# GNN layer and FFN in one kernel: outer weights loaded by rows, phase 3's opening in a fixed order, unused transposes in FFN's first waits, chunk 0's layernorm by two engines

## The chip, the core and the metric

One core of one Trainium2 chip runs the whole program. The metric is the device time of one execution in microseconds (us); the median of three runs is compared. TensorE (PE) multiplies and transposes, VectorE (DVE), ScalarE (ACT) and GpSimd (POOL) do elementwise work, SyncE (SP) issues most DMAs. All data are 32-bit floats; a matmul of such data shows as two records on PE, a transpose as one.

## The reference

`x` has 10000 rows (nodes) of 512, and there are 5000 edges with 64 attributes each.

```python
edge_index = jnp.stack([src, dst])
x = x + gnn(layernorm(x), edge_attr_64, edge_index, W_e, b_e, W1, ...)
x = x + ffn(layernorm(x)[None], controller, f1, f2)[0]

def gnn(x, edge_attr, ...):
    msg = relu(x[src] + edge_attr @ W_e + b_e)
    h = (1.0 + eps) * x + segment_sum(msg, dst, num_segments=x.shape[0])
    h = silu(bn(h @ W1 + b1, g1, beta1))          # 512 -> 1024
    h = h @ W2 + b2                               # 1024 -> 512
    return silu(bn(h, g2, beta2))                 # bn: over all nodes, per column

def ffn(x, controller, f1, f2):                   # groups of 16 tokens, 16 experts x 4 sets
    logits = einsum('bgtd,des->bgtes', grouped, controller) + tie
    perm = (logits == max over the 16 tokens)     # one token per group, expert and set
    inner = relu(einsum over t of (grouped @ f1) with perm)      # f1: 512 x (64 * 32)
    return einsum('bgesd,bgtes->bgtd', inner @ f2, perm)         # f2: (64 * 32) x 512
```

## The kernel before, in words

*Phase 1* (to about 200 us) gathers the edges' source rows, computes messages and adds them to `agg` in HBM. *Phase 2* (to 744 us) computes `h @ W1` for ten pairs of 500-node blocks, *phase 3* (to 1228 us) `h @ W2` for the same ten pairs, *FFN* (to the end) works on 20 chunks of 512 nodes.

Both products are done by Strassen's scheme with seven products instead of eight: `weight_sums` makes five sums of weight quarters (u1, u2, u5, u6, u7) on DVE, `block_sums` makes sums of data quarters (s1, s3, s6 on POOL, s4, s7 on DVE), and `strassen` runs products 1 to 7 for one output block `m`, each over `kb` pieces (2 in phase 2, 4 in phase 3), in PSUM banks x, w, z, y, v; products 6 and 7 add to the banks of 3 and 1. Products 2 and 5 read the data itself and u2 and u5; 3 and 4 read w2 itself and s3 and s4. The order of the products is a tuple (`FIRST`, (2, 5, 4, 3, 1, 6, 7), for the first output block of a phase).

Between phase 2 and 3 stands batchnorm 1. Phase 2's last pair keeps its four result pieces in SBUF (`xt`, `at`); phase 3 starts with this pair. For each piece `m`, `bn1` aggregates the statistics (bn_aggr on DVE), takes the root (two operations on POOL) and makes scale and shift (three on DVE), and ACT applies SiLU in place (L420). Piece 3 is the last to be ready. The weight sums for phase 3 read `w2` (L106, w_u in the profile). The other nine pairs are loaded from `h1s` in HBM, into `hc` or into `xt` and `at`.

In FFN a chunk's four tiles of 128 tokens go through these steps: `load_y` (yt, from `h2s`), `load_x`, `silu` (ACT, on yt), `residual` (four transposes of yt on PE into a bank, an addition on DVE), `stats` (bn_stats and bn_aggr on DVE), `norm` (four small operations on POOL, then per tile one scaling into `xl`, on POOL), `flip` (transposes of xl, a copy by ACT to `xlt`), `logits`, `choose` (three DVE operations), `by_token` (two transposes, then products into `bd` on DVE), `gather` (PE, copied by ACT to `gs`), `inner` (PE, with the inner weights `f1`), `relu`, and one step later `outer` (PE, with the outer weights `f2`), `turn` (DVE transposes) and `scatter`. A function `step` writes one order for four chunks at a time: `a` is at flip to by_token, `b` at gather to relu, `d` at outer, `e` at turn and scatter; `n1`, `n2` are the next two. `InOrder` keeps every operation of an engine in the program's order, so FFN's order is the one that is written; in phases 2 and 3 a scheduler places what is not marked with `keep_in_program_order`. A pool's tile is free again when its last reader is done: that decides when a load may be issued. SP issues its DMAs one after the other. All of FFN's operations on the engines show as L529, so the trace is read by tiles there. yt and x of chunk 0 are loaded early into a pool of their own; the other FFN tiles lie where phase 3's were.

FFN begins with `load_y`, `load_x` and `silu` of chunks 0 and 1, the loads of f1, then residual and stats of chunk 0, its norm, three residuals of chunk 1, and `step` for chunk 0 alone. Then the loads of f2 follow, in eight parts of 32 partitions:

```python
for q in range(2):
    for h in range(2):
        for t in range(2):
            rows = slice(64 * q + F * h, 64 * q + F * (h + 1))
            nc.sync.dma_start(out=f2_to[rows, :, t, :], in_=f2[h, q, :, :, t, :])
```

Of the kernel before, what the change touches and what calls it, by code (L numbers as in the profile page):

```python
# [20 lines left out]
EPS = 1e-5  # L21

P = 128
# [22 lines left out]
NP = NB // 2  # L46
FIRST = (2, 5, 4, 3, 1, 6, 7)


@with_exitstack  # L50
def gnn_ffn_kernel(ctx: ExitStack, tc: tile.TileContext, a: dict, out: bass.AP):
# [24 lines left out]
    def batchnorm(name, stats, blocks, g, beta):  # L76


        mv = const.tile([P, blocks, 2], F32, name=name + "_mv")
        sc = const.tile([P, blocks], F32, name=name + "_sc")  # L80
        sh = const.tile([P, blocks], F32, name=name + "_sh")

        def part(ms):
            for m in range(blocks)[ms]:
                nc.vector.bn_aggr(out=mv[:, m, :], in_=stats[:, m, :, :].rearrange("p c s -> p (c s)"))
            x = sc[:, ms]
            nc.gpsimd.tensor_scalar(x, mv[:, ms, 1], EPS, None, op0=ALU.add)
            nc.gpsimd.tensor_tensor(x, x, power[:, ms, 0], ALU.pow)
            nc.vector.tensor_mul(x, x, g[:, ms])
            nc.vector.tensor_mul(sh[:, ms], mv[:, ms, 0], x)  # L90
            nc.vector.tensor_sub(sh[:, ms], beta[:, ms], sh[:, ms])

        return sc, sh, part
# [4 lines left out]

    def weight_sums(pool, name, w, kb, mh):

        def q(i, j):
            return w[:, j * kb:(j + 1) * kb, i * mh:(i + 1) * mh]

        def f(n, x0, x1, op):
            t = pool.tile([P, kb, mh], F32, name=f"{name}_u{n}")
            tc.keep_in_program_order(nc.vector.tensor_tensor(t, x0, x1, op))  # L106
            return t

        u2 = f(2, q(1, 0), q(1, 1), ALU.add)
        u5 = f(5, q(0, 0), q(0, 1), ALU.add)  # L110
        u1 = f(1, q(0, 0), q(1, 1), ALU.add)
        u7 = f(7, q(0, 1), q(1, 1), ALU.subtract)
        u6 = f(6, q(1, 0), q(0, 0), ALU.subtract)
        return {1: u1, 2: u2, 3: q(0, 0), 4: q(1, 1), 5: u5, 6: u6, 7: u7}

    def block_sums(pool, name, kb, q):


        r = {n: [q(i, i, k, k + 1)[:, 0] for k in range(kb)] for n, i in ((2, 0), (5, 1))}
        for n, eng, x0, x1, op in ((3, nc.gpsimd, (0, 1), (1, 1), ALU.subtract),  # L120
                                   (1, nc.gpsimd, (0, 0), (1, 1), ALU.add),
# [4 lines left out]
            r[n] = [t[:, k, :] for k in range(kb)]  # L126
            for k0, k1 in [(0, kb)] if q(0, 0, 0, kb) is not None else [(k, k + 1) for k in range(kb)]:
                eng.tensor_tensor(t[:, k0:k1], q(*x0, k0, k1), q(*x1, k0, k1), op)  # L128
        return r

    def strassen(ps, tmp, us, bs, kb, m, res, bias0, bias1, y, order=(3, 1, 2, 5, 4, 6, 7)):


        banks, kept, done = {}, {}, set()

        def product(n, bank, start):
            for k in range(kb):
                nc.tensor.matmul(bank, lhsT=us[n][:, k, m * P:(m + 1) * P], rhs=bs[n][k],  # L138
                                 start=start and k == 0, stop=k == kb - 1, skip_group_check=True)

# [4 lines left out]
        def part(name, x0, sc, x1, op, dst=None):  # L145
            if dst is None:
# [9 lines left out]
                ({4, 5, 7}, lambda: part(None, 7, bias0, "t1", ALU.add, res[:, 0, 0, :]))]  # L156
        names = {2: ("w", 1), 5: ("v", 1), 4: y, 3: ("z", 2), 1: ("x", 2)}
        for n in order:
            if n in names:
                banks[n] = ps.tile([P, TB], F32, name=names[n][0], bufs=names[n][1])  # L160
# [176 lines left out]
    with tc.tile_pool(name="p2", bufs=1) as p2, tc.tile_pool(name="ps_2", bufs=1, space=PSUM) as ps_2:  # L337
# [86 lines left out]
        for i in range(NP):  # L424
# [4 lines left out]
            for m in range(4):  # L429
# [15 lines left out]
                else:  # L445

                    bn1(slice(m, MH, 4))
                    for r, t in ((0, slice(0, 2)), (1, slice(0, 2))) if m < 3 else (
                            (0, slice(0, 1)), (1, slice(1, 2)), (1, slice(0, 1)), (0, slice(1, 2))):
                        silu(h1[:, r, t, :].rearrange("p t n -> p (t n)"), 4 * r + m)  # L450
                if more and 0 < m < 3:
# [12 lines left out]
    with tc.tile_pool(name="pb", bufs=1) as pb, tc.tile_pool(name="ps_3", bufs=1, space=PSUM) as ps_3:  # L464
        u2 = weight_sums(pb, "w2", w2, 4, H // 2)
        for o, i in enumerate([NP - 1, *range(NP - 1)]):
            if o > 0:
# [4 lines left out]
                for m in range(4):  # L472
                    for r in range(2):
                        silu(pieces[m][:, r].rearrange("p t n -> p (t n)"), 4 * r + m)
            bs = block_sums(pb, "h", 4, lambda r, t, k0, k1: pieces[k0][:, r, t:t + 1, :] if k1 == k0 + 1 else None)
            for m in range(2):
                h2 = pb.tile([P, 2, 2, TB], F32, name="h2", bufs=2)
                strassen(ps_3, pb, u2, bs, 4, m, h2, b2[:, m:m + 1], b2[:, 2 + m:3 + m], ("y", 2),
                         *((FIRST,) if o == m == 0 else ()))
                for r in range(2):  # L480
# [12 lines left out]
    for t in range(2):  # L493
        for u in range(4):
            for b in range(2):
                nc.vector.tensor_copy(
                    ctl.rearrange("p k (t u q s b) -> p t u b k q s", t=2, u=4, q=2, s=2)[:, t, u, b],
                    ctl_in.rearrange("p k (u b q t s) -> p t u b k q s", t=2, u=4, q=2, s=2)[:, t, u, b])

# [33 lines left out]
    class Chunk:  # L533
# [61 lines left out]
        def norm(self):  # L595
# [8 lines left out]
            for j, (_, m, _) in enumerate(self.tiles):  # L604
                xl = pf.tile([P, H], F32, name="xl", bufs=8)
                pool.tensor_scalar(xl[:m, :], self.row_tile(j)[:m, :], self.rs[:m, j, :], self.sh[:m, j, :],
                                        op0=ALU.mult, op1=ALU.add)
                self.xl.append(xl)
# [73 lines left out]
        def inner(self, k, gs):  # L682
# [5 lines left out]
            for m in range(MF):  # L688
                for q in range(2):
                    b, t = m // 2, m % 2  # L690
                    j = 4 * b + 2 * q + t
                    pe.matmul(self.pi[64 * q:64 * q + 64, m], lhsT=f1_sb[:, k, 2 * F * j:2 * F * (j + 1)],
# [107 lines left out]
    def step(a, b, d, e, n1, n2):  # L800
# [36 lines left out]
        def silu(k):  # L837
            if n1 and n1.c == 2:
                n1.silu(k)
            if n2 and n2.c > 2:  # L840
                n2.silu(k)

        m1 = n1 if n1 and n1.c > 1 else None
        put(m1, Chunk.load_x)
        put(e, Chunk.split)
# [38 lines left out]
        lo(3)  # L884
        put(a, Chunk.choose)
        res(m1, 0)
        put(d, Chunk.outer, 2)
        res(m1, 1)
        put(a, Chunk.by_token)
        put(d, Chunk.outer, 3)  # L890
        stats(m1, 0)
# [10 lines left out]
    for k in range(KH):  # L902
        nc.sync.dma_start(out=f1_sb[:, k, :], in_=a["L0_ffn_f1"][k * P:(k + 1) * P, :])
    for j in range(4):
        chunks[0].residual(j)
        chunks[0].stats(j)
    chunks[0].norm()
    for j in range(3):
        chunks[1].residual(j)
        if j < 2:  # L910
            chunks[1].stats(j)
    step(at(0), None, None, None, at(1), at(2))

    f2 = a["L0_ffn_f2"].rearrange("(b q t s f) d -> s q f b t d", s=2, q=2, t=2, f=F)
    f2_to = f2_sb.rearrange("p (b t) d -> p b t d", t=2)
    for q in range(2):
        for h in range(2):
            for t in range(2):
                rows = slice(64 * q + F * h, 64 * q + F * (h + 1))
                nc.sync.dma_start(out=f2_to[rows, :, t, :], in_=f2[h, q, :, :, t, :])  # L920
    for c in range(1, NC):
# [96 lines left out]
```

## Time and profile before

| | us |
|---|---|
| median of 3 runs (lowest, highest) | 1945.13 (1942.31, 1946.38) |
| the profiled execution: time, span | 1945.13, 1943.3 |
| PE busy | 1798.0 (93%) |
| DVE busy | 1200.9 (62%) |
| ACT busy | 720.9 (37%) |
| POOL busy | 628.9 (32%) |
| mean granted clock of TensorE | 0.969 |

The span runs from the first to the last instruction; what lies around it is 1.8 us. In the 40 slices of the page each digit is the busy share of a slice (48.6 us) in tenths; PEclk is the granted clock in tenths of full speed. "idle before <-X" names the engine and line that ended a wait, inferred from semaphores. PEld are weight loads, which overlap matmuls.

### The profile page before, as it was taken

Reading aid. Unit: us, or ns where it says so; the run is one execution under the profiler, and the core shown is the slowest. Engines: PE = TensorE matmul, PEld = TensorE weight load, DVE = VectorE, ACT = ScalarE, POOL = GpSimd, SP = SyncE. Lnnn points to the kernel's source line nnn. Section 1 sums busy time; section 2 is a strip of 40 time slices with the busy share of each in tenths; the row PEclk is TensorE's granted clock in tenths of the full one; section 3 lists DMA queues with packets and bytes.
Section 4 is the critical chain, followed back from the end, with each engine's and each line's share of the span. In section 5 each row is a group of like instructions: output and inputs, shape, how many; then the busy total and the mean of one; then the engine's idle time right before and its main releaser. Section 6 shows DMA issues by size and latency. Waiting matters only on the chain.

```text
span 1943.3 us, 43938 instructions
## 1 busy us (share of the span) xinstructions
PE 1798.0 (93%) x19354; PEld 1032.9 (53%) x19354; DVE 1200.9 (62%) x1904; ACT 720.9 (37%) x970; POOL 628.9 (32%) x638
## 2 busy tenths in 40 slices
PE   4969499999999997999999999789999999999997
PEld 2424244444444443444444444466867677777764
DVE  7536367777777767343433334416878786868777
ACT  0324233333333233222222220255656555555543
POOL 4275433333233224333333332122232323232332
PEclk9979699999999998999999999789999999999999
DMA  9997444443444312333333331652232323323101
GB/s 349 304 233 144 109 172 171 162 162 148 162 162 163 145 43 85 127 148 126 127 136 139 127 127 42 212 157 68 90 111 90 108 93 101 100 97 94 58 25 58
DMA packets 95217, 256.35 MB, mean 132 GB/s; under 512 B 7845, under 2 KB 8435, under 8 KB 94452
## 3 DMA queue, kind: packets, MB, share of 16 engines
q1 hardware_dynamic: 86068, 232.58, 32.8%
q0 software_dynamic: 8960, 20.98, 5.4%
q8 instruction: 151, 2.47, 0.5%
q14 instruction: 38, 0.31, 0.1%
HBM read 143.47 MB, written 110.07 MB: 130 GB/s over the span
## 4 chain that ended last, share of the span: by engine, by line
PE 68%; DVE 10%; DMA 7%; ACT 5%; POOL 4%; SPq 3%; issue 2%; POOLq 0%; DVEq 0%; ACTq 0%
PE pb L529 16%; PE pi L529 10%; PE x L138 9%; PE z L138 9%; PE w L138 5%; PE v L138 5%; PE ps L529 4%; PE y L138 3%; SPq L217 3%; PE pc L309 2%; DVE ln_st L360 2%; ACT xt L371 2%; DVE st L442 2%; DMA L_ffn_controller_sb<-in_L_ffn_controller_dram 2%; ACT it L529 2%
## 5 line engine op out<-in xcount | busy, mean ns | idle before, releaser
L138 PE MATMUL x<-h_s,w_u 128*128 128x500 f32 x640 | 287.9, 582 | 0.3 <-POOL h_s L128 0.3
L529 ACT COPY gs<-pb 128x1024 f32<-128x1024 f32 (+2 forms) x168 | 161.6, 1027 | 120.1 <-PE pb L529 115.6
L138 PEld LDWEIGHTS x<-h_s,w_u 128*128 128x128 f32 x640 | 121.5, 190 | 147.3 <-issue 142.3
L529 DVE STREAM_TRANSPOSE it<-it 128x1024 f32<-128x1024 f32 x152 | 175.0, 1210 | 0.1
L529 PE MATMUL pi<-gs,f_sb 128*64 128x64 f32 x5120 | 167.4, 226 | 0.9 <-issue 0.9
L529 PEld LDWEIGHTS pi<-gs,f_sb 128*64 128x64 f32 x5120 | 158.7, 141 | 8.9 <-issue 1.9
L529 PE MATMUL pb<-bd,xl 32*128 32x128 f32 x2504 | 145.4, 287 | 12.6 <-ACT it L529 8.8
L529 POOL TENSOR_TENSOR pv<-perm,odd_t 64x512 f32<-64x512 f32 (+1 forms) x80 | 99.9, 1248 | 174.9 <-PE pb L529 152.6
L148 DVE SCALAR_TENSOR_TENSOR t<-w,s 128x500 f32<-128x500 f32 x60 | 40.7, 678 | 183.9 <-PE w L138 176.4
L138 PE MATMUL z<-h_s,w 128*128 128x500 f32 x320 | 147.6, 583 | 4.1 <-POOL h_s L128 4.1
L138 PE MATMUL z<-h_s,w_u 128*128 128x500 f32 x320 | 144.0, 582 | 0.3 <-POOL h_s L128 0.3
L529 PEld LDWEIGHTS pb<-bd,xl 32*128 32x128 f32 x2504 | 129.8, 189 | 25.2 <-ACT it L529 13.6
L529 DVE COPY it<-pb 128x1024 f32<-128x1024 f32 x72 | 88.2, 1225 | 83.4 <-PE pb L529 83.4
L529 PE MATMUL pb<-f_sb,ib 32*32 32x256 f32 x4864 | 132.5, 385 | 6.8 <-ACT it L529 4.7
L128 POOL TENSOR_TENSOR h_s<-hc 128x500 f32<-128x500 f32 x60 | 77.0, 1318 | 152.0 <-PE z L138 152.0
L529 ACT COPY it<-pb 128x1024 f32<-128x1024 f32 x76 | 79.6, 1047 | 104.1 <-PE pb L529 104.1
L143 ACT COPY s<-z 128x500 f32<-128x500 f32 x60 | 34.5, 575 | 213.8 <-PE z L138 164.6
L529 POOL TENSOR_SCALAR ln_rs<-ln_mv 128x4 f32<-128x4 f32 (+2 forms) x22 | 5.0, 226 | 304.1 <-DVE ln_mv L529 294.2
L138 PEld LDWEIGHTS z<-h_s,w_u 128*128 128x128 f32 x320 | 60.7, 190 | 74.0 <-issue 72.2
L128 POOL TENSOR_TENSOR h_s<-hb 128x1000 f32<-128x1000 f32 x30 | 69.6, 2335 | 87.0 <-PE z L138 65.3
L442 DVE BATCH_NORM_STATS2 st<-h 128x6 f32<-128x500 f32 x144 | 93.7, 671 | 1.3
L529 PEld LDWEIGHTS pb<-f_sb,ib 32*32 32x32 f32 x4864 | 68.8, 103 | 45.8 <-issue 12.8
(190 smaller groups left out, 3118.7 us busy)
## 6 DMA issues: line engine op xcount, KB each, us to landing
h1s<-h SPq DMA_DIRECT2D x36, 1000.0 KB
agg<-zero SPq DMA_DIRECT2D x10, 2048.0 KB
xt<-in_x_dram SPq DMA_DIRECT2D x20, 1000.0 KB
hc<-h1s SPq DMA_DIRECT2D x20, 1000.0 KB
h2s<-h SPq DMA_DIRECT2D x20, 1000.0 KB
x<-in_x_dram SPq DMA_DIRECT2D x39, 512.0 KB
out_dram<-x SPq DMA_DIRECT2D x39, 512.0 KB
yt<-h2s SPq DMA_DIRECT2D x76, 256.0 KB
```

Source lines behind the costliest of these rows:

```text
L128: eng.tensor_tensor(t[:, k0:k1], q(*x0, k0, k1), q(*x1, k0, k1), op)
L138: nc.tensor.matmul(bank, lhsT=us[n][:, k, m * P:(m + 1) * P], rhs=bs[n][k], start=start and k == 0, stop=k == kb - 1, skip_group_check=True)
L143: nc.scalar.copy(kept[n], banks[n])
L148: nc.vector.scalar_tensor_tensor(dst, banks[x0], sc, kept[x1], op0=op, op1=ALU.add)
L217: nc.sync.dma_start(out=agg[r0:r0 + j * P, :].rearrange("(p j) d -> p j d", j=j), in_=zero.to_broadcast([P, j, H]))
L309: nc.tensor.matmul(pc, lhsT=same[k][:, i, :], rhs=xgs[g * EG + k], start=(k == i), stop=(k == EG - 1))
L360: tc.keep_in_program_order(nc.vector.bn_stats(out=st[:RT, j, :], in_=self.xt[:RT, j, :]))
L371: keep(nc.scalar.activation(r, r, AF.Identity, bias=self.sh[:RT, j, :], scale=self.rs[:RT, j, :]))
L442: nc.vector.bn_stats(out=st1[:, 4 * r + m, 2 * i + t, :], in_=h1[:, r, t, :])
L529: return lambda *args, **kw: tc.keep_in_program_order(f(*args, **kw))
```

## The change

- *Outer weights*: f2 is loaded as it lies, 128 rows to the 128 partitions, in four DMAs of 1 MB. The place of two indices (set bits t and q) is swapped in `ctl` and in `inner`, so that the inner results stand in the order of these rows.
- *Phase 3's opening*: the sums for the first three pieces, then u2 and u5, then batchnorm's small operations and SiLU for piece 3, then the other sums, then u1, u7, u6 are written in this order. For the first output block TensorE runs products 4, 3, 2, 5 on three pieces each, then on the fourth piece each, then 1, 6, 7.
- *Unused transposes*: `keep_going(n)` transposes the identity n times into a bank that nobody reads: 24 ahead of chunk 0's first residual, 4 behind each of the seven residuals, 8 behind choose and 6 behind by_token of chunk 0.
- *Chunk 0's layernorm*: the scaling of tiles 1 and 3 is done by ACT, that of 0 and 2 by POOL.
- *Chunk 2*: x is loaded ahead of f2 (it was behind), and its four SiLUs stand ahead of step 1 (they stood amid it, one each before those of chunk 3).

```diff
+LATER = (4, 3, 2, 5, 1, 6, 7)
...
-        def part(ms):
...
+        def root(ms, keep=lambda x: x):
...
+        def rest(ms, keep=lambda x: x):
...
-    def weight_sums(pool, name, w, kb, mh):
+    def weight_sums(pool, name, w, kb, mh, between=lambda: None):
...
         u5 = f(5, q(0, 0), q(0, 1), ALU.add)
+        between()
         u1 = f(1, q(0, 0), q(1, 1), ALU.add)
...
+        def rest():
+            for n in (3, 1, 4, 6, 7):
+                for eng, *args in todo[n]:
+                    f = eng.tensor_tensor(*args)
+                    if between:
+                        tc.keep_in_program_order(f)
+
+        if between:
+            for n in (3, 4):
+                while len(todo[n]) > 1:
+                    eng, *args = todo[n].pop(0)
+                    tc.keep_in_program_order(eng.tensor_tensor(*args))
+            between(rest)
...
+        for n in order[:early]:
+            banks[n] = ps.tile([P, TB], F32, name=names[n][0], bufs=names[n][1])
+            product(n, banks[n], True, range(kb - 1))
         for n in order:
-            if n in names:
+            if n in banks:
+                product(n, banks[n], False, [kb - 1])
+            elif n in names:
...
+                    else:
+                        bn1.root(slice(m, MH, 4), tc.keep_in_program_order)
...
+            def last_block():
+
+                bn1.rest(slice(3, MH, 4), tc.keep_in_program_order)
+                for r, t in ((0, 0), (1, 1), (1, 0), (0, 1)):
+                    silu(pieces[3][:, r, t, :], 4 * r + 3)
+                others()
...
-                         *((FIRST,) if o == m == 0 else ()))
+                         *((LATER, 4) if o == m == 0 else ()))
...
-                    ctl_in.rearrange("p k (u b q t s) -> p t u b k q s", t=2, u=4, q=2, s=2)[:, t, u, b])
+                    ctl_in.rearrange("p k (u b t q s) -> p t u b k q s", t=2, u=4, q=2, s=2)[:, t, u, b])
...
+                if self.c == 0 and j % 2:
+                    act.activation(xl[:m, :], self.row_tile(j)[:m, :], AF.Identity, bias=self.sh[:m, j, :],
+                                   scale=self.rs[:m, j, :])
...
-                    j = 4 * b + 2 * q + t
+                    j = 4 * b + 2 * t + q
...
-            if n1 and n1.c == 2:
-                n1.silu(k)
...
-        put(m1, Chunk.load_x)
+        if m1 and m1.c > 2:
+            m1.load_x()
...
         put(a, Chunk.choose)
+        if a and a.c == 0:
+            keep_going(8)
...
         put(a, Chunk.by_token)
+        if a and a.c == 0:
+            keep_going(6)
...
+    def keep_going(n):
+
+        idle = ps_b.tile([P, 2, 2, HD], F32, name="pb")
+        for i in range(n):
+            pe.transpose(idle[:, 0, 0, :P], ident, ident)
+
+    keep_going(24)
     for j in range(4):
         chunks[0].residual(j)
         chunks[0].stats(j)
+        keep_going(4)
     chunks[0].norm()
     for j in range(3):
         chunks[1].residual(j)
         if j < 2:
             chunks[1].stats(j)
+        keep_going(4)
     step(at(0), None, None, None, at(1), at(2))
...
+    chunks[2].load_x()
+    for k in range(KH):
+        chunks[2].silu(k)
+
+    for m in range(0, MF, 4):
+        nc.sync.dma_start(out=f2_sb[:, m:m + 4], in_=a["L0_ffn_f2"][m * P:(m + 4) * P, :].rearrange("(m p) d -> p m d", p=P))
```

## Prediction

> **What bounds the kernel now.** I read the slices first. They say that TensorE is busy 93% of the span, so only the stretches where it is not can pay; the clock row has its dips at the same places.
>
> ```profile
> PE   4969499999999997999999999789999999999997
> ...
> PEclk9979699999999998999999999789999999999999
> ```
>
> Slice 16 (the opening of phase 3) and slices 25 to 27 (FFN's opening) are the two places that the diff touches. The windows give their size (columns: stretch, its length, busy time of PE, PEld, DVE, ACT, POOL, granted clock, DMA share, GB/s).
>
> ```profile
> 740.00:760.00 20.00, 9.80 (x22) 3.55 (x20) 16.47 (x20) 0.82 (x2) 13.87 (x11) 0.90 0.51 206
> 1240.00:1260.00 20.00, 14.37 (x76) 8.43 (x77) 6.86 (x15) 3.92 (x6) 4.72 (x8) 0.59 1.04 352
> 1260.00:1300.00 40.00, 30.88 (x450) 25.37 (x452) 9.72 (x21) 18.09 (x24) 4.73 (x8) 0.77 0.70 179
> 1300.00:1400.00 100.00, 96.74 (x2432) 75.16 (x2432) 67.51 (x96) 57.69 (x69) 30.56 (x38) 1.00 0.27 87
> ```
>
> From 1300 on FFN runs at full clock; before that it runs at 0.59 and 0.77. Next the timeline of the two places, and the chain of waits, which shows what ended last in them.
>
> ```profile
> 760.03 8.90 DVE L106 TENSOR_TENSOR w_u<-w 128x1024 f32<-128x1024 f32 x5
> 761.29 2.03 PE L138 MATMUL w<-xt,w_u 128*128 128x500 f32 x2 [7.28 <-DVE w_u L106]
> 761.72 6.13 POOL L128 TENSOR_TENSOR h_s<-at 128x500 f32<-128x500 f32 x3 [1.63 <-ACT at L420]
> 1243.71 3.01 POOL L529 TENSOR_SCALAR xl<-x,ln_rs,ln_sh 128x512 f32<-128x512 f32 x4
> 1257.30 2.67 PE L529 MATMUL pb<-bd,xl 32*128 32x128 f32 x32 [0.52 <-DVE bd L529]
> 1281.13 5.04 ACT L529 ACTIVATE yt<-yt,bn_sh,bn_sc 128x512 f32<-128x512 f32 x7 [3.88 <-DMA yt<-h2s]
> 1288.05 1.12 PE L529 MATMUL pi<-xlt,ctl 128*64 128x256 f32 x4 [5.27 <-ACT xlt L529]
> ```
> ```profile
> 1264.87 16.23 DMA yt<-h2s
> 1281.13 2.09 ACT yt L529 x3
> ```
>
> In phase 3, TensorE waits 7.28 us for weight sums that DVE starts only after everything else. In FFN, chunk 3's yt lands at 1281.1; ACT then does seven SiLUs, and TensorE stands 5.27 us.
>
> **The change, part by part.** The sum is made on the profiled execution: 1945.13 us, of which 1943.3 is span; the median of the runs is the same 1945.13. About 0.2% (3.9 us) is what a measurement here can tell from no change.
>
> *Opening of phase 3.* Phase 2's last matmul ends at 743.97; nine of the 28 matmuls of the first output block then wait or run at half clock; from 766.38 on TensorE never stops, and the block ends at 782.4. A matmul is two records of 0.419 us, 0.84 us, so 28 cost 23.5 us; the stretch takes 38.4: 14.9 us are lost. After the change:
> - DVE: the last bn_stats ends about 746.7, two bn_aggr of 0.69 end at 748. POOL's root (0.23 and 0.72) now stands ahead of its sums, ready at 749.0 instead of 754.3, but the sums queued behind it start at 749 instead of 746.1.
> - DVE makes three s4 pieces (0.67 alone, up to 1.7 beside POOL: 748.0 to 750.4), then u2 and u5. Five w_u took 8.90 with POOL beside most of them; the four beside it took 7.7, or 1.93 each: until 754.3. POOL's first three s3: 1.67 to 2.04 each, until 754.7. The three small operations took 1.19 each beside POOL and 0.16 alone; POOL now stands idle, so they end about 755.5, against 760.1.
> - ACT: four SiLUs of 0.72, until 758.6. One SiLU on prefetched hc is queued ahead of them; hc's four loads moved from 747.5 to 757.7, the first has landed by about 751, so it is done in time.
> - POOL then has nine sums left (s3's last, s1, s6), where it had three left before: 1.67 each beside DVE's sums, 2.04 beside w_u, 1.2 alone: until about 774. DVE has five sums (1.64 contended) and u1, u7, u6: until about 772.
> - TensorE does y, z, w, v on three pieces each as these arrive (748.7 to about 761), even at half clock in time; the four last pieces until 764 to 766.5; then it waits for u1 (about 768), then for s6's last piece (774). That product ends about 775, the last 3.35 later: 778.
>
> So 782.4 becomes about 778: **-4.5 us**. If POOL runs as if alone (1.2) the block ends at 774 (-8); with every sum at 2.04, 781.5 (-1).
>
> *FFN, clock.* The one-microsecond windows give the clock's changes at 1233.9, 1254.4, 1257.8, 1268.1, 1274.9, 1278.3, 1285.1 and 1291.9: all multiples of 3.41 us apart, so I asked for stretches of that length (TensorE's busy time stands behind the length).
>
> ```profile
> 752.65:756.06 3.41, 1.36 (x4) 0.32 (x2) 1.67 (x2) 0.00 (x0) 3.41 (x4) 1.00 0.99 415
> 1227.10:1230.50 3.40, 1.66 (x5) 0.46 (x3) 2.17 (x4) 0.00 (x0) 0.00 (x0) 1.00 0.02 9
> 1271.50:1274.90 3.40, 1.89 (x32) 1.81 (x32) 0.00 (x0) 0.31 (x1) 0.00 (x0) 1.00 1.05 204
> 1295.40:1298.80 3.40, 2.92 (x40) 2.40 (x41) 3.26 (x9) 0.69 (x1) 0.00 (x0) 1.00 0.02 2
> ```
>
> Behind the first (1.36 us of TensorE) the clock fell, behind the second (1.66) it held. The question is whether transposes count. The third had 1.89 us of gather matmuls (32 rows) alone, and it fell; the fourth had 1.7 of the same and 1.2 of transposes, and it held. So they count, and I take it that 24 of them (0.165 each at full clock, from 0.66 for four: 4.0 us), filling 1229.3 to 1233.3, and four after each residual hold the clock. They cost nothing while the clock holds: eight transposes take 1.32 per tile, and DVE beside them 1.53 (0.66+0.69+0.18); the eight before by_token fit in choose's 1.5; the six before the first gather cost up to 0.5.
>
> [...]
>
> *FFN, steps at full clock.*
> - Chunk 0's LN: four xl of 0.75 on POOL become two, with two on ACT, idle then (its copies wait until 1247.29): -1.5.
> - Flips and logits: 1247.92 to 1254.84 is 6.9 at half clock. Three flips of 0.66 and four logits of 0.65 are 4.6, with a wait for the last copy 4.8: -2.1; perm's transposes -0.2. The first gather starts about 1253.6 instead of 1257.30.
> - Gathers and inner matmuls of chunk 0: 1257.30 to 1281.76, 24.5. The next chunk's, at full clock, take 15.7 (1296.9 to 1312.6). Two gaps of 1.5 and 0.9 by "issue" may stay: -6.4 to -8.8. Chunk 0's end then lies at 1269.3 to 1271.5.
> - Outer weights: the windows show 7.4 MB moved by 1254 (yt and x of chunk 1, the inner weights, yt of chunk 2 make 7.3), then 0.20 MB/us at full DMA share until 1276, then 0.39 for x and yt. The fall lies where the loads with 32 partitions run; by whole rows of 128 partitions I take 0.39, as x and yt have (bounds 0.20 and 0.43). x of chunk 2 ahead of them and yt of chunk 3 behind then end at about 1254+6.2/0.39 = 1270, not 1281.1. At 0.20 nothing would be won there. On SP's queue four issues stand where eight took 13.76 us.
> - Chunk 2's SiLUs move ahead of the gs copies; 3 us of work while ACT stood idle (1253.91 to 1258.98). yt lands piece by piece until about 1253.8. Chunk 3's four then end by 1271.
> - From chunk 0's last inner matmul to the next logits took 6.3; relu (1.38 on DVE, 1.19 on ACT) and a copy of 0.58 alone make it 3.4. So 1288.05 becomes 1272.7 to 1275, and the logits behind it gain up to 0.7.
>
> Sum for FFN: -13 to -16, less 0.5 for the six transposes: **-13.5**. Later steps are bound by TensorE and only shift. The swapped index of ctl, the inner weights and f2 gives the same instructions with other addresses: nothing.
>
> Total 1945.1 - 4.5 - 13.5 = **1927**.
>
> **The rivals.**
> - *The transposes do not hold the clock.* Then they cost: eight per tile at half clock are 2.1 against DVE's 1.53, seven tiles in order on TensorE, and the first flip ends 2.4 us later, hiding the LN gain; the eight and the six add 1.6. Gather 4 us later, inner matmuls as before less at most 2.4 of gaps; then 2.9 is given back at the SiLUs. FFN: -1.3 to +1.1. Time 1939.5 to 1942, say 1940.5. For it: no window of the trace holds transposes alone. 18%.
> - *Slower: chunk 2's SiLUs block ACT.* ACT is in order; behind them stand the gs copies, and behind these the gathers. Were yt of chunk 2 to share the queue with x and f2 behind it, the next logits would come about 19.3 us after its last piece (0.8 and 15.1 of gathers and inner matmuls, then 3.4). From a landing at 1273 on it costs more than phase 3 brings; the trace bounds the landing only by when these SiLUs ran, the first at 1276.42, the last after 1284. With the last piece at 1279 the logits come at 1298.3: FFN +10.3, phase 3 -4.5, total 1951. Against it: the bytes, and chunk 1's pieces, for which ACT waited in turn (1236.4 to 1239.8). 6%.
> - *Half of it:* the clock falls once amid the gathers, or the loads of instructions make gaps while the DMA engines are full (more work per microsecond is fetched now): 4 to 8 us less, 1931 to 1936. 16%.
>
> **The numbers.** The clock holds: 60%, 1927, own range 1921 to 1931 (phase 3 from -8 to -1, FFN from -16 to -13). Range 1920 to 1941: it takes in the third rival and most of the first, and leaves out the rest of that and the second. Slower by over 0.2%: most of the second rival, 5%. Within 0.2% (above 1941.2): a part of the first and the rest of the second, 8%. Faster: 87%.
>
> **What would show it.** Right: first gather near 1249 (1253.6 less phase 3's 4.5) with the clock at 1.00 from phase 3's end on; DMA near 390 GB/s until about 1265; no ACT wait for yt; the first output block of phase 3 over 34 us after phase 2's last matmul, not 38.4. Wrong: clock 0.5 behind the 24 transposes; gs copies behind a wait for yt; or POOL's nine sums lasting past 778.

## Result and the profile after

The changed kernel takes 1927.61 us (median; 1925.84 to 1928.31) beside 1944.42 for the kernel before: 0.9914 of it, 95% interval 0.9899 to 0.993. The forecast was 1927.0. The sum came out; not all of its steps did.

The profiled execution has a span of 1926.6 us, 16.7 less than before. Cut at seven points that both traces have, it divides as follows (times in us):

| stretch | before | after | difference |
|---|---|---|---|
| start to phase 2's last matmul | 743.96 | 744.52 | +0.56 |
| to the end of phase 3's first output block | 38.35 | 34.48 | -3.87 |
| to phase 3's last matmul | 446.16 | 446.16 | 0 |
| to the first gather | 28.83 | 25.08 | -3.75 |
| gathers and inner products of chunk 0 | 24.46 | 20.70 | -3.76 |
| to the next logits | 6.29 | 3.37 | -2.92 |
| to chunk 1's last inner product | 24.59 | 23.79 | -0.80 |
| the steps behind it, and the end | 630.66 | 628.50 | -2.16 |

The slices of the page (TensorE's busy share and its granted clock, in tenths) show the same two places as before, counted from 1: slice 16 rises from 7 to 8 in busy share and from 8 to 9 in clock, slice 26 from 7 to 8 and from 7 to 9, slice 27 stays at 8 in both:

```profile
PE   4959499999999998999999999889999999999997
...
PEclk9969699999999999999999999989999999999998
```

The windows (length, busy time of PE, PEld, DVE, ACT, POOL, clock, DMA share, GB/s):

```profile
740.00:760.00 20.00, 15.15 (x31) 6.28 (x30) 16.73 (x23) 6.47 (x9) 8.05 (x6) 0.83 0.52 205
1240.00:1260.00 20.00, 15.09 (x167) 11.48 (x168) 6.17 (x14) 10.71 (x14) 6.63 (x12) 0.88 1.03 400
1260.00:1300.00 40.00, 36.49 (x771) 31.14 (x778) 10.24 (x21) 21.41 (x27) 9.88 (x13) 0.93 0.41 147
```

Read them with the row for 1300 on, unchanged in kind: FFN's opening runs at 0.88 and 0.93 instead of 0.59 and 0.77, not at 1.00. The DMA engines move 400 GB/s between 1240 and 1260 (352 before), and 97 between 1272 and 1274, when the loads are nearly through.

The timeline of phase 3's opening and of FFN's (the line of POOL is from the view of POOL alone):

```profile
750.18 3.40 DVE L116 TENSOR_TENSOR w_u<-w 128x1024 f32<-128x1024 f32 x2
753.51 1.20 DVE L93 TENSOR_TENSOR bn_sc<-bn_sc,L_gnn_g_sb 128x2 f32<-128x2 f32 x1
766.92 3.59 PE L167 MATMUL x<-h_s,w_u 128*128 128x500 f32 x8 [1.50 <-DVE w_u L116]
771.30 4.52 PE L167 MATMUL z<-h_s,w_u 128*128 128x500 f32 x8 [0.79 <-DVE w_u L116]
773.41 1.24 POOL L145 TENSOR_TENSOR h_s<-at 128x500 f32<-128x500 f32 x1
1226.09 2.81 PE L582 MATMUL pb<-ident 128*128 128x128 f32 x24 [0.92 <-DVE h L179]
1250.24 1.72 PE L582 MATMUL pb<-bd,xl 32*128 32x128 f32 x32
1254.41 3.01 PE L582 MATMUL pb<-bd,xl 32*128 32x128 f32 x32 [1.86 <-ACT gs L582]
1274.31 0.65 PE L582 MATMUL pi<-xlt,ctl 128*64 128x256 f32 x4 [2.33 <-ACT xlt L582]
```

Phase 3: the 7.28 us wait for weight sums is gone; what is left are 1.50 and 0.79 us, for DVE's u1 and u6, and short waits inside product 6 (4.52 us where eight records without a wait take 3.52): its last three pieces each begin 0.05 to 0.06 behind the end of a sum of GpSimd, the last at 774.71, behind the one shown, which ends at 774.66. Product 7 then runs without a wait, so GpSimd's last sum sets the block's end. FFN: the first gather starts at 1250.24; the second, which needed only a bank of the first, waits 1.86 us for a copy by ACT. The chain of waits tells why:

```profile
1235.81 14.69 DMA yt<-h2s
...
1250.52 2.93 ACT yt L582 x4
1253.45 0.92 ACT gs L582
...
1254.41 3.01 PE pb L582 x32
```

In ACT's program order chunk 2's four SiLUs stand ahead of the copies. Their yt was there only at 1250.5, so nothing of the 2.93 us was done while ACT had been idle, and the first copy began at 1253.4. Behind that wait the clock fell. These are stretches of 3.41 us that end where the clock changes (columns as above):

```profile
1228.05:1231.46 3.41, 1.67 (x12) 1.05 (x11) 0.48 (x3) 2.22 (x3) 0.45 (x1) 1.00 0.54 196
1231.46:1234.87 3.41, 3.41 (x17) 3.41 (x18) 2.81 (x5) 1.52 (x2) 0.00 (x0) 0.50 0.93 297
1251.92:1255.33 3.41, 1.55 (x22) 1.32 (x20) 2.23 (x5) 3.37 (x5) 0.27 (x2) 1.00 1.05 387
1255.33:1258.74 3.41, 3.41 (x48) 3.19 (x46) 0.00 (x0) 2.08 (x2) 3.13 (x6) 0.50 1.06 387
1258.74:1262.15 3.41, 3.41 (x56) 3.29 (x54) 0.00 (x0) 0.00 (x0) 1.35 (x2) 0.50 1.04 385
```

Behind a stretch with 1.67 us of TensorE the clock fell, behind one with 3.41 it was back. Behind 1.55 us it fell again, and two full stretches of gathers and inner products ran at 0.50.

### The profile page after: what moved, and what is told of

Read it like the earlier page. It is cut to its first block, busy times and chain, and to the rows that moved or that the text cites. A ratio compares the mean times of both kernels' runs of the same rounds, so it can differ in the third digit from the quotient of the medians.

```text
span 1926.6 us, 44074 instructions
## 1 busy us (share of the span) xinstructions
PE 1793.8 (93%) x19420; PEld 1034.4 (54%) x19420; DVE 1202.6 (62%) x1904; ACT 722.5 (38%) x972; POOL 632.0 (33%) x636
## 3 DMA queue, kind: packets, MB, share of 16 engines
q8 instruction: 152, 2.49, 0.5%
## 4 chain that ended last, share of the span: by engine, by line
PE 68%; DVE 9%; DMA 7%; ACT 5%; POOL 4%; SPq 4%; issue 3%; POOLq 0%; DVEq 0%; ACTq 0%
PE pb L582 16%; PE pi L582 11%; PE x L167 9%; PE z L167 9%; PE v L167 5%; PE w L167 5%; PE ps L582 3%; SPq L253 3%; PE y L167 3%; PE pc L345 3%; DVE ln_st L396 2%; ACT xt L407 2%; DVE st L478 2%; ACT it L582 2%; DMA L_ffn_controller_sb<-in_L_ffn_controller_dram 2%
## 5 line engine op out<-in xcount | busy, mean ns | idle before, releaser
L174 ACT COPY s<-z 128x500 f32<-128x500 f32 x60 | 34.5, 576 | 216.2 <-PE z L167 166.6
L407 ACT ACTIVATE xt<-xt,ln_sh,ln_rs 125x512 f32<-125x512 f32 x80 | 59.5, 805 | 91.5 <-POOL ln_sh L403 91.5
```

What stands on the lines that cost most here:

```text
L174: nc.scalar.copy(kept[n], banks[n])
L407: keep(nc.scalar.activation(r, r, AF.Identity, bias=self.sh[:RT, j, :], scale=self.rs[:RT, j, :]))
```

## The experiments

All kernels are derived from the changed one. The ratio is to the kernel before, timed beside each. The stages are from each profiled execution: "opening" from phase 2's last matmul to the end of phase 3's first output block; the next four in us behind phase 3's last matmul; "rest" from chunk 1's last inner product to the end; "half" is how many clock stretches of 3.41 us ran at 0.50 in the first 45 us behind phase 3's end. The median of the kernel before was 1945.01 in the set with e1, e2, e3 and e5, 1945.56 in that with e6 to e9 (on another chip) and 1942.86 in that with e10 to e13, so between sets the ratios compare better than the times.

| kernel | time | ratio, interval | opening | first gather | chunk 0's last inner | next logits | chunk 1's last inner | rest | half |
|---|---|---|---|---|---|---|---|---|---|
| before | 1944.42 | 1 | 38.4 | 28.8 | 53.3 | 59.6 | 84.2 | 630.7 | 9 |
| changed | 1927.61 | 0.9914 (0.9899-0.993) | 34.5 | 25.1 | 45.8 | 49.2 | 72.9 | 628.5 | 3 |
| e1 no transposes | 1933.45 | 0.9937 (0.992-0.9953) | 34.5 | 27.3 | 48.7 | 52.1 | 74.7 | 630.9 | 9 |
| e2 f2 to 32 rows | 1935.49 | 0.9959 (0.9944-0.9975) | 34.5 | 24.7 | 52.5 | 57.8 | 82.8 | 625.1 | 2 |
| e3 SiLUs put back | 1928.20 | 0.9914 (0.9898-0.9931) | 34.4 | 26.2 | 44.0 | 48.6 | 72.8 | 627.4 | 1 |
| e5 phase 3 only | 1943.79 | 0.9989 (0.9979-0.9998) | 34.5 | 28.5 | 54.0 | 60.5 | 85.0 | 631.4 | 9 |
| e6 40 transposes | 1928.53 | 0.991 (0.9894-0.9927) | 34.4 | 26.2 | 44.2 | 47.6 | 71.4 | 631.8 | 2 |
| e7 SiLUs spread | 1925.16 | 0.9892 (0.9876-0.9909) | 34.5 | 24.7 | 42.1 | 47.0 | 70.8 | 628.4 | 1 |
| e8 product 7 first | 1924.76 | 0.9889 (0.9872-0.9905) | 31.7 | 24.7 | 45.7 | 49.0 | 72.9 | 628.1 | 2 |
| e9 LN by GpSimd | 1926.97 | 0.9899 (0.9882-0.9915) | 34.5 | 28.5 | 45.9 | 49.3 | 74.3 | 628.6 | 2 |
| e10 transposes early | 1927.00 | 0.9915 (0.9899-0.9931) | 34.6 | 27.4 | 47.4 | 50.7 | 74.5 | 625.0 | 9 |
| e11 both (e7, e8) | 1923.22 | 0.9891 (0.9876-0.9907) | 31.7 | 27.1 | 44.8 | 48.2 | 72.2 | 629.6 | 3 |
| e12 third | 1919.40 | 0.988 (0.9863-0.9897) | 31.7 | 24.7 | 42.4 | 45.8 | 68.4 | 626.2 | 1 |
| e13 both, no transposes | 1928.12 | 0.9921 (0.9907-0.9936) | 31.7 | 27.3 | 48.5 | 51.9 | 74.5 | 630.2 | 9 |

**e5, phase 3 alone.** The kernel with all of FFN as before and only phase 3's opening changed: f2 by 32 rows, chunk 2's SiLUs behind the gathers, LN by GpSimd, no transposes.

> The kernel before with the new opening of phase 3 alone; FFN is that of before. Theory: from phase 2's last matmul to the end of phase 3's first output block 34.5 us instead of 38.4, all of it kept: time 3 to 5 us below before. Rival (given back later in phase 3, where DVE and POOL have more left to do): the block ends early but phase 3 as a whole is no shorter; time within 1 us of before.

The opening is 34.45 us, and phase 3 ends 3.9 sooner behind phase 2's last matmul. In the time 1.2 us are left: FFN up to chunk 1's last inner product took 0.8 more and the rest 0.8 more in this trace. So phase 3 brings what it was to bring in its place, but in the time neither the 3 to 5 us of the theory nor the rival's less than 1; FFN's program is the same as before, so the 0.8 us of each of these two stages is a difference between two executions of it.

**e1, no transposes.**

```diff
     def keep_going(n):
-        idle = ps_b.tile([P, 2, 2, HD], F32, name="pb")
-        for i in range(n):
-            pe.transpose(idle[:, 0, 0, :P], ident, ident)
+        return
```

> The changed kernel without its 66 unused transposes. From phase 3's last matmul to the first gather of chunk 1 took 68.4 us before and 57.3 in the changed kernel. Theory (the transposes hold the clock): the clock falls about 5 us behind phase 3's end, as before, and stays at 0.5 through flips and logits (6.9 us instead of 4.4) and most of the gathers and inner matmuls (over 22 us instead of 20.7): this stretch is 61 to 64 us, the time 3 to 6 us above the changed kernel. Rival (transposes don't count as activity, the clock was held by something else): the stretch is 57 to 58 us, the time the same or 0.5 us less.

The clock goes to 0.50 for nine stretches, as before the change, and yet the next logits come only 2.9 us later than in the changed kernel and chunk 1's last inner product 1.8. Chunk 1's first gather comes 59.1 us behind phase 3's end, below the theory's 61 to 64 and above the rival's 57 to 58. Without the transposes the residuals and statistics do not get slower, since VectorE sets their pace, busy 1.90 to 1.93 of every 2 us from 1234.2 to 1242.2 (the flips begin at 16.1 us, 16.3 in the changed kernel), and the first gather, later now, has its copies behind no SiLU that still waits. But the time is 5.8 us up, and its interval overlaps the changed kernel's a little. The trace's other 3.3 us lie where no transpose stands: 2.4 in the rest, 0.9 ahead of FFN.

**e10, the same 66 transposes elsewhere.** To learn what those microseconds hang on, 66 transposes were put at the head of phase 3, where TensorE waits anyway, and none in FFN.

```diff
         first = {}
+        idle = ps_3.tile([P, TB], F32, name="w", bufs=1)
+        for i in range(66):
+            tc.keep_in_program_order(nc.tensor.transpose(idle[:, :P], ident, ident))
...
```

> The changed kernel without its 66 unused transposes in FFN's opening, but with 66 of them at the head of phase 3, where TensorE waits 4.8 us (7 us of transposes: they may push phase 3's opening from 34.5 to as much as 37). The kernel without transposes lost 5.8 us, of which its trace shows 1.8 between phase 3's end and chunk 1's last inner product and 2.4 in the twenty steps and the tail behind it. Theory: that second part hangs on where TensorE's instructions stand in its stream (66 more of them ahead of the steps: 627.4 to 628.6 us for what follows chunk 1's last inner product in all but one kernel that has them; none or 82: 630.7 to 631.8), not on what they do; with 66 placed elsewhere it is 627 to 629 again, while chunk 1's last inner product stays at 74 to 76 after phase 3's end. Rival: it is a matter of TensorE's clock as FFN begins; then it stays at 630.5 to 631.8.

FFN's opening stays as in e1 (74.5, nine stretches at half speed), and the rest is 625.0, below the forecast 627 to 629; the time is the changed kernel's, 1927.0 (ratio 0.9915 beside 0.9914). So by the medians most of what the transposes are worth in the time is not the clock in FFN's first waits. In phase 3 they cost nothing, though they delayed its first product by 6.3 us (11.1 behind phase 2's last matmul instead of 4.8):

```profile
746.08 9.06 PE L506 MATMUL w<-ident 128*128 128x128 f32 x66 [2.18 <-DVE at L179]
754.98 2.68 PE L167 MATMUL y<-h_s,w 128*128 128x500 f32 x6
```

The six records (three matmuls) behind them ran at full clock (2.68, against 4.89 at 749.30 in the changed kernel), and the opening took 34.6.

**e13, both improvements without transposes**, beside e11 below in one set of runs.

> As the kernel with both, without the 66 unused transposes. Theory: they are worth 4 to 6 us in all (1.5 to 2.5 of it between phase 3's end and chunk 1's last inner product, the rest behind it, as in the first kernel without them): 1926.5 to 1928.5. Rival: only what the stretch shows is theirs, and the rest of the 5.8 us was chance: 1 to 2.5 us, 1923.5 to 1925.

4.9 us above e11, as the theory had it (4 to 6); the traces show 2.3 of it up to chunk 1's last inner product. Over all kernels the rest is 625.0 to 629.6 with 66 transposes, wherever they stand, and 630.2 to 631.8 with none or with 40 at the head. Most of that spread, however, goes with the clock near the program's end. In the rest a step of one chunk takes 32.79 us, and some take 0.1 to 3.0 more, the longest where one or two half-speed stretches begin 50 to 88 us ahead of the end. Behind the last inner product the program takes another 35.9 to 36.3 us in e2, e3 and e10 and 38.5 to 39.4 in all others, and only in these others does a half-speed stretch begin 19 to 22 us ahead of the end. Of the 5.9 us by which e10's rest is shorter than e1's, 3.1 lie there and 1.6 in the long step; the remaining 1.2 is spread over several steps. Whether the transposes have a part in where the clock falls so late is not shown.

The shorter of the long steps have gaps by "issue" inside runs of like matmuls, in the stretch from 76 to 632 us behind phase 3's end 2.1 us of them before and 0.7 after. Their ends go with the packets of one DMA queue: q8 of the page, of kind "instruction", moves 2.49 MB in 152 packets, 16 KB each. From 20 us behind phase 3's end on, all 36 gaps of 0.2 us or more in the 14 traces end 1.2 to 1.6 us behind the landing of such a packet. That TensorE waits there for its instructions is inferred from this alone. Why there are such gaps in some steps and not in others stays open: that 66 transposes more or fewer shift the packets against the work was the author's guess, and e12 has TensorE's instructions in e11's order, and none of its steps is long.

**e6, 40 transposes at the head.**

```diff
-    keep_going(24)
+    keep_going(40)
```

> One number is changed: 40 unused transposes instead of 24 at the head of FFN (at 0.11 us each they last until about 1230.5, where 24 ended at 1228.9). Theory: TensorE is then busy for more than 2.5 of the 3.4 us before its clock is set anew, so the half-speed window of the changed kernel (6.6 to 10 us after phase 3's last matmul) is gone, but the stretch to the first gather goes by VectorE's residual sums and statistics, so the first gather stays at 25.1 us after phase 3's end, within 0.6, and the time at 1927.6 within 1. Rival: the half-speed window sets the pace of the residuals; the first gather comes 1.5 to 2 us sooner and the time is 1925.5 to 1926.

The half-speed stretch at 6.3 us is gone, and little is gained by it: VectorE was pacing the residuals, as the theory said, and the flips begin at 15.9 instead of 16.3. The clock fell later instead, once behind the wait for chunk 0's LN (17.9 to 21.3 us) and once amid the inner products, and the first gather came 1.1 later, which the theory did not have. Chunk 1's last inner product came 1.5 sooner, and the rest took 3.3 more. The time is within its spread of the changed kernel's.

**e9, LN by GpSimd.**

```diff
-                if self.c == 0 and j % 2:
+                if self.c < 0:
```

> Chunk 0's layer norm goes back to GpSimd alone (four tiles of 0.76 us each in a row instead of two beside ScalarE's two); all else as in the changed kernel. Theory: the last tile is written 1.5 us later, the flips, logits and gathers move with it: first gather 26.4 us after phase 3's last matmul instead of 25.1, the second chunk's logits 1 to 1.5 us later, time 1928.5 to 1929.2. Rival: the 1.5 us is taken up again by the chunk 2 SiLUs, which wait for their transfer until 1250.5 whatever comes before: the first gather's copies then start when they did, logits at 49.2, time 1927.6 within 0.7.

The first gather is 3.5 us later (the clock fell behind the later LN and was at 0.50 from 1243.2 to 1250.0), more than either side had. What LN by two engines is worth at the same clock shows without the transposes: the first gather at 27.3 in e1, 28.8 in the kernel before, 1.5 apart. And yet chunk 0's inner products end when they did, at 45.9 and 45.8 us. The gather's copies start at 29.8 behind phase 3's end instead of 28.2, now without a wait for yt:

```profile
1250.33 2.93 ACT L582 ACTIVATE yt<-yt,bn_sh,bn_sc 128x512 f32<-128x512 f32 x4
1254.87 1.99 ACT L582 COPY gs<-pb 128x1024 f32<-128x1024 f32 x2 [1.61 <-PE pb L582]
```

The time is the changed kernel's within its spread. LN by two engines, as it stands here, brings nothing that shows in the time: the copies behind it wait for another transfer.

**e3, chunk 2's SiLUs put back** behind the gathers, each ahead of chunk 3's.

```diff
         def silu(k):
+            if n1 and n1.c == 2:
+                n1.silu(k)
...
     chunks[2].load_x()
-    for k in range(KH):
-        chunks[2].silu(k)
```

> The changed kernel with chunk 2's four SiLUs put back amid step 1, behind the copies of the gathers, one each before those of chunk 3. Theory (in the changed kernel they wait for yt and keep the first gather's copies and so TensorE waiting, and the clock falls): no wait of the second gather for ACT, the clock holds, gathers and inner matmuls of chunk 0 take 16 to 17 us instead of 20.7; but eight SiLUs then stand before relu's half on ACT, so the next logits gain only 0 to 2 us, time -2 to +1. Rival (TensorE is held by its instruction loads or the DMA engines): gathers and inner matmuls stay at 20 us or more, and the eight SiLUs add 2 to 3 us.

Gathers and inner products take 17.7 us against 20.7, all of it at full clock; the one half-speed stretch, at 18 us, lies ahead of them. Then eight SiLUs stand in front of the relu, and the next logits gain 0.5. The time is the same: this part of the change moves the wait from one end of the gathers to the other.

**e7, the SiLUs spread**, two behind the third gather and two behind the fourth.

```diff
         gat(2)
+        first(0)
+        first(1)
         inn(1)
...
         turns(6, 8)
+        first(2)
+        first(3)
...
```

> Chunk 2's four SiLUs are issued two behind the third gather and two behind the fourth, neither all ahead of the first gather's copies (the changed kernel) nor all in front of the relu with chunk 3's (the kernel with the SiLUs put back). Theory: ScalarE had 2.1 us idle between the gathers' copies, so these hide; the gathers and inner products take 17 to 18.5 us as with the SiLUs put back (17.7), not 20.7, and only chunk 3's four stand in front of the relu, so that the second chunk's logits start 46.5 to 47.6 us after phase 3's last matmul instead of 49.2 (changed kernel) or 48.6 (put back); time 1925 to 1926.5. Rival: whatever is won in the gathers is lost again in front of the logits, because chunk 3's SiLUs wait for their own transfer; logits at 48.6 or later, time 1927 to 1928.5.

17.4 us for gathers and inner products, the next logits at 47.0: as the theory had it; 1925.16 us. The interval (0.9876 to 0.9909) still overlaps the changed kernel's; the stage shows the mechanism.

**e2, the outer weights to 32 rows at a time**, in the new row order.

```diff
-    for m in range(0, MF, 4):
-        nc.sync.dma_start(out=f2_sb[:, m:m + 4], in_=a["L0_ffn_f2"][m * P:(m + 4) * P, :].rearrange("(m p) d -> p m d", p=P))
+    f2_by = a["L0_ffn_f2"].rearrange("(m p) d -> p m d", p=P)
+    for r in range(4):
+        for m in range(0, MF, 8):
+            nc.sync.dma_start(out=f2_sb[32 * r:32 * r + 32, m:m + 8], in_=f2_by[32 * r:32 * r + 32, m:m + 8])
```

> The changed kernel with the outer weights loaded in eight parts of 32 partitions, as before, into the new order of rows. Theory: the DMA engines move 0.20 MB/us during these loads instead of 0.39, for 21 us instead of 11; chunk 3's yt lands some 10 us later, ACT waits for it, and the next chunk's logits come 5 to 8 us later than in the changed kernel; time +5 to +8 us. Rival (the rate before was low for another reason, such as full queues): 0.39 MB/us and the same time.

The window of 1255 to 1270, then the timeline with TensorE amid the inner products and ACT's next SiLUs:

```profile
1255.00:1270.00 15.00, 13.96 (x266) 13.03 (x266) 0.19 (x2) 6.81 (x7) 4.76 (x8) 0.77 1.07 205
```
```profile
1273.40 4.96 PE L582 MATMUL pi<-gs,f_sb 128*64 128x64 f32 x86 [4.29 <-issue]
1278.84 2.93 ACT L582 ACTIVATE yt<-yt,bn_sh,bn_sc 128x512 f32<-128x512 f32 x4 [9.63 <-DMA yt<-h2s]
```

205 GB/s at full share, where whole rows of 128 had 385 to 389. Chunk 3's yt makes ACT wait 9.63 us, and TensorE stands 4.29 in the middle of a run of like matmuls, where the profile shows nothing that it waits for; the gap ends 1.5 us behind the landing of an instruction packet (see e13). At this place it is 1.27 in e3 and e12. With the loads by 32 partitions it was 2.38 in e5 and 1.51 in the kernel before, one gather earlier. The next logits come 8.6 us later than in the changed kernel, the time is 7.9 up. This is the largest single part of the change, and all of it shows in the stage, where chunk 1's last inner product comes 9.8 later.

**e8, product 7 ahead of product 6** in phase 3's opening, with u1 and u7 ahead of VectorE's s7.

```diff
-LATER = (4, 3, 2, 5, 1, 6, 7)
+LATER = (4, 3, 2, 5, 1, 7, 6)
...
-        between()
+        later = between()
         u1 = f(1, q(0, 0), q(1, 1), ALU.add)
         u7 = f(7, q(0, 1), q(1, 1), ALU.subtract)
+        if later:
+            later()
...
-                others()
+                others((3, 1, 4, 6))
+                return lambda: others((7,))
...
```

> Phase 3's opening only: VectorE forms u1 and u7 ahead of its four sums s7 and u6 behind them, and TensorE takes product 7 ahead of product 6, whose block sums GpSimd finishes last (774.65 in the profiled run). Theory: TensorE's waits for VectorE's u1 (1.50 us) and u6 (0.79) go, and a short wait for the copy of product 1's bank comes in; the stretch from phase 2's last matmul to the end of the first output block falls from 34.5 to 31.8 to 32.8 us and the time by about 2, to 1925.0 to 1926.5. Rival: GpSimd's chain of sums is the bound whatever the order, and the added contention of VectorE's long sums makes it later still: 34.0 to 35 us, time 1927 to 1928.5.

The opening falls to 31.7: the block ends 32.5 us behind phase 2's last matmul, but one matmul of the second block (0.84) now stands ahead of that. One wait is left, for GpSimd's last sum for product 1 (0.54), and GpSimd's very last one, ready at 775.4, is no longer what the block's end waits for:

```profile
766.06 2.69 PE L169 MATMUL x<-h_s,w_u 128*128 128x500 f32 x6
769.28 1.10 PE L169 MATMUL x<-h_s,w_u 128*128 128x500 f32 x2 [0.54 <-POOL h_s L147]
```

The 2.8 us last to phase 3's end (477.8 us behind phase 2's last matmul, 480.6 in the changed kernel). The time is 1924.76; its ratio, 0.9889, is below the changed kernel's 0.9914, with overlapping intervals.

**e11 and e12, put together.** e11 has e7's and e8's edits. e12 moves chunk 3's four SiLUs behind the flips too:

```diff
-            if n2 and n2.c > 2:
+            if n2 and n2.c > 3:
                 n2.silu(k)
...
         fl(3)
+        if n2 and n2.c == 3:
+            for k in range(KH):
+                n2.silu(k)
...
```

> The changed kernel with product 7 ahead of product 6 in phase 3's opening and chunk 2's SiLUs two by two behind the third and fourth gather. Theory: both gains add up, as they lie 450 us apart: phase 3's opening 31.7, the second chunk's logits at 46.5 to 47.5 after phase 3's end, time 1927.6 - 2.8 - 2.4 = 1922.4, within 1.2. Rival: what the SiLUs gave in their run (1925.2) was where the clock's windows happened to lie; then only phase 3's gain stays, 1924.8 within 0.8.

> As the kernel with both, and chunk 3's four SiLUs are issued behind the flips of the second chunk, no longer ahead of the relu. Theory: from the last inner product of chunk 0 to the next logits it takes 3.4 us (as in the changed kernel) instead of 4.9, the second chunk's logits start at 45 to 46.2 after phase 3's end, time 0.8 to 1.5 below the kernel with both. Rival: ScalarE has the SiLUs to do in any case before the third chunk's residuals, and they now delay the copies of the later flips; same time within 0.6.

e11: 1923.22, within the theory's range, while its next logits at 48.2 are not. Its opening is 31.7, but in its trace, that of the slowest of its four executions (1926.50), the clock fell for two stretches amid the logits (17 to 24 us), and the first gather came at 27.1. Its ratio, 0.9891, is that of e7 (0.9892) or e8 (0.9889) alone, so that the two gains add up in the time is not shown. e12: 1919.40, the fastest, 3.8 below e11 where the theory had 0.8 to 1.5; its interval (0.9863 to 0.9897) ends just below that of the changed kernel. ACT is now free when the inner products end, and waits for TensorE and VectorE:

```profile
1260.37 1.52 ACT L585 ACTIVATE yt<-yt,bn_sh,bn_sc 128x512 f32<-128x512 f32 x2
1265.95 1.19 ACT L585 ACTIVATE ib<-pi 32x512 f32<-32x512 f32 x2 [4.06 <-DVE ib L585]
```

From the last inner product to the next logits it takes 3.36 us, as in e11 (in e7 4.86, where the inner products ended sooner and the SiLUs did not). Of the 8.0 us between the two traces 2.4 are the clock in e11's logits and 3.4 lie in the rest; that moving chunk 3's SiLUs is worth anything beside e11 is not shown beyond the intervals. Beside e7 the stage shows it, in one trace each: with the same first gather, 24.7, the next logits come 1.2 sooner.

## Why the prediction was right, and where it was not

- *Phase 3's opening*, -4.5 forecast, -3.87 measured, and e5 has the same with nothing else changed. The mechanism was right: the wait that takes over is for GpSimd's nine sums, said to last until about 774 and product 6 until about 775; they lasted until 774.66, and product 7 followed at 775.65. The wait for u1 was foreseen too (about 768; it ended at 766.9). What the working had wrong cost little: the three small operations of the batch norm's rest were put at 0.16 because GpSimd would stand idle, and two took 1.20 and 1.16, as GpSimd was still at its third sum until 755.9; the wait of 0.79 for u6 was not foreseen, and ends ahead of the sums of GpSimd that product 6 needs in any case. e8, which puts product 7 into the wait for those sums, brought another 2.8.
- *The first gather* was to come at 1253.6 instead of 1257.30, 3.7 sooner behind phase 3's end; it came 3.75 sooner. Its parts came out as well: LN by two engines 1.5 (e1 against the kernel before, at the same clock), flips to first gather at full clock 2.5 (8.8 us, 11.3 in e1), forecast 2.3. But the 1.5 of LN is not seen in the time (e9), because the copies behind the first gather wait for yt's SiLUs in any case.
- *Gathers and inner products*, -6.4 to -8.8 forecast, -3.76 measured: the step that failed. It took it that yt of chunk 2 lands piece by piece and that ACT does these SiLUs while it stands idle. All four ran in a row from 1250.5 on, ahead of the copies. That is the second rival's mechanism in the small, as the landing was 1250.5 and not 1273 or later; behind the 1.86 us of TensorE's wait came the third rival's fall of the clock, to 0.50. e3 has this stage at 17.7 and e7 at 17.4, inside the forecast's 15.7 to 18.1, though these too hold a gap of 1.3 by "issue" that the forecast allowed for; in the changed kernel that gap is not there. Nor was most of what this stage did gain the clock: without the transposes, with three half-speed stretches in it as before, it took 21.4 us (e1) against 24.5.
- *From the last inner product to the next logits*: 3.4 forecast, 3.37 measured. The load by whole rows, taken at 0.39 MB/us, ran at 0.385 to 0.389, and e2 shows what the old rate costs: this stretch 5.3, and ACT 9.63 us of waiting for chunk 3's yt.
- *The clock*: 24 transposes were costed at 0.165 each and 4.0 us; they took 0.11 each and ended at 1228.9, so the first wait was not filled and one stretch ran at half speed. It cost 0.4 us at most (16.3 us to the first flip; 15.9 to 16.1 in all other kernels). Behind transposes alone the clock rose: the stretch 1231.46 to 1234.87 held nothing else, at 0.50, and the next was at 1.00. Without the unused ones it fell more often: e1 has nine half-speed stretches instead of three. So the first rival is out.
- *What the clock is worth* was sized far too high. About 8.7 us of FFN's 13.5 were put on it (2.1, 0.2 and at least 6.4). But e1 and e10, with nine half-speed stretches as before, have chunk 1's last inner product at 74.7 and 74.5 us behind phase 3's end, against 84.2 before and 72.9 in the changed kernel: the clock brings 1.8 of the 11.2 us, and 3.7 with e7's order of the SiLUs (70.8, against 74.5 in e13). e2, with the transposes but with the outer weights by 32 partitions, has it at 82.8. The load by whole rows is what pays here: in e2 the first gather comes at 24.7, as early as in any kernel, and the gain is lost again behind it.
- *The sum* agrees with the time better than its steps do. FFN's opening gave 11.2 of the 13.5 us up to chunk 1's last inner product; another 1.6 came from stretches that the forecast held for unchanged (+0.56 and -2.16), and the latter spreads by up to 6.8 between these kernels, for the most part by where the clock falls near the end. That is luck for the forecast and no part of its argument.

## What to carry to other kernels

Before moving work ahead of an in-order engine's other work, ask for the landing of its last operand and for what is queued behind: here ACT's 3.51 us of idle time before 1250.5 went unused, and the SiLUs' wait for yt became one of 1.86 us for TensorE. The best place for such work is the idle time between the copies (e7), found by reading that engine's waits in the profile. When a wait ends, read which operand came last before reordering: in phase 3 exchanging two products and their sums gained 2.8 us in that stage on top of the 3.9 of the change. And before a gain is put down to one of several parts, take that part out alone: the clock had most of the forecast, and e1 leaves it 1.8 us of FFN's opening.

## What had not been expected of the hardware

- Busy time alone does not say whether the clock falls: 1.66 us of 3.40 held it in the kernel before (phase 3's last products), 1.67 of 3.41 let it fall in the changed one. At half speed one full stretch of transposes brought it back (1231.46 to 1234.87); in the changed kernel one of 32-row gathers and inner products did not (1255.33 to 1258.74, busy 3.41 of 3.41), and the next, again of both, did, while in e6 one stretch (about 1257.5 to 1261), nearly all of it inner products, was enough.
- The stretches lie on a grid that does not follow the program. In the changed kernel's trace, from 94.83 to 1914.13, a whole number of stretches of 3.41 us lies between each change of the clock and the next (the 477.87 us at full clock from 753.60 on are 140 of them). The changed kernel and e8 have the same FFN; one had three half-speed stretches (from 6.3 and from 30.2 us behind phase 3's end), the other two (from 29.9). e7 and e11, also alike in FFN, had one and three, and the first gather at 24.7 and 27.1. The clock fell behind stretches in which TensorE was not idle, but worked for 1.67 and 1.55 us (from 1228.05 and 1251.92 in the changed kernel).
- All 36 of TensorE's gaps of 0.2 us or more that the profile calls "issue", in FFN from 20 us on, end 1.2 to 1.6 us behind the landing of a 16 KB packet of the instruction queue, from which it is inferred that its instructions were late. With the DMA engines full of transfers at 0.20 MB/us the longest was 1.51 (before), 2.38 (e5) and 4.29 us (e2), with 0.39 MB/us 1.58 (e1) or less.
- VectorE's and GpSimd's sums of data in SBUF took longer side by side. In the changed kernel's opening of phase 3 a GpSimd sum of 128x500 took 1.24 us with none of VectorE's beside it, 1.64 to 1.71 beside VectorE's block sums and 2.22 to 2.27 beside its weight sums; VectorE's of the same size took 0.67 at 749.01, ahead of GpSimd's first, and 1.72 to 1.75 beside GpSimd's.
